# Summing quarters of softmax denominators on VectorE instead of TensorE, in a two-layer image kernel

## The chip, the cores and the metric

The kernel runs on one core of a Trainium2 chip, in float32. The metric is device time in microseconds (us), the median of several executions. TensorE (PE) multiplies matrices, VectorE (DVE) and GpSimd (POOL) do elementwise work, ScalarE (ACT) does activations and copies, SyncE (SP) issues the transfers. Each engine works through a queue of its own in a fixed order; a value that comes from another engine is waited for with a semaphore, and everything behind a waiting instruction in the same queue waits too.

## The reference

The input x has 4 images of 512 channels and 64x64 pixels (4096 pixels, called N). Layer 0 is self-attention with a residual, layer 1 an involution (a convolution whose weights differ from pixel to pixel) with a residual:

```
q = wq @ x + bq ; k = wk @ x + bk ; v = wv @ x + bv      # 128 channels each
attn = softmax(q^T k, axis=-1)                           # 4096 x 4096
x = wo @ (v @ attn^T) + bo + x                           # 512 channels
o = relu(W1 @ x * s1 + b1)                               # 128 channels
w = Ws @ relu(Wr @ o * sr + br) + bs                     # 8 groups x 49 taps
o = sum over 7x7 patch of w * patch(o)                   # per pixel and group of 16 channels
x = W3 @ o * s3 + b3 + x
```

## The kernel before

**Attention.** An image is worked in 8 blocks (c = 0 to 7) of 512 pixels as queries. A block has 32 steps, one for each 128 keys. In a step PE makes scores (`pss`) and ACT takes their exponentials straight from PSUM (`pt`, L797); two steps later PE multiplies the exponentials with the values into `po` (L820), and DVE adds them into a running sum `pacc` (L826 for the first, L828, and L831 for the last, whose result is `sums`). Nothing is divided until the block is over. After every step `chores` (L308) lets three generators go on by one step each: `finish_block` (what is left to do for the attention block before), `close_chunk` (the end of the involution for a block), and, paced by a planner's clock, `involution` (the taps). A bare `yield` in a generator is thus one step of the attention, a pause of n steps is n of them. The planner keeps a clock `pe` of the matmul work, and an estimate `free` of when DVE, POOL and the transfers will be done; `takes` (L211) books an instruction there. A tap is put into the program only where these estimates are not too far ahead of the clock.

**finish_block (L636 to 776).** `on` is the copy of `po` from PSUM. `sums` (128 partitions x 512 pixels) has to be summed over its partitions. DVE's `tensor_reduce` with a transpose (L654) gives `blocks`, 128 x 16: partition p = 32 i + a holds the part that quarter i of the partitions contributes to pixel a of each of the 16 groups of 32 pixels. The four quarters still have to be added. After a pause of 3 steps (L657) a matmul with `quads`, a matrix of repeated 32x32 identities, does this into a PSUM tile `pl` (L658 to 660), and every quarter receives the whole sum. DVE takes the reciprocal from PSUM into `rl` (L663), spreads it by a block transpose into a PSUM tile `spread` (L666), and multiplies `on` by it (L670). After another pause of 5 steps (L686) follow the four matmuls of the output projection `pwo` with their residual adds on DVE (L679), then the first 1x1 convolution of the involution (`p1`, ReLU to `o1`, L699), a transpose to pixel order (`o1t`, L732), its transfer to DRAM (`pix`), and the reduced weights (`pr`, `red`, L757). The last image (`late`) takes other waits, by the planner's clock, and computes the transposes on PE.

**Involution.** Sixteen units of 4 image rows for each image. A unit first makes its weights `pw` on PE. For each tap DVE multiplies a piece of the ring of image rows with the weights (`prod`, L427) and POOL adds the product into `acc` (L447); two folds on POOL end the unit (L462). `turn_unit` (L497) then transposes `acc` on DVE (`turned`, L508), writes it to DRAM (L517), and for every second unit reads it back as `accT`. `close_chunk` (L568) multiplies it by W3 in four matmuls `py` (L575), one every two steps; each is followed by the residual update of `x` on DVE (L577), and the transfer of the block to the output ends it (L586).

**PSUM.** The pool `ps` has two buffers for the tag "mm" (L127). All of `pl`, `spread`, `pwo`, `p1`, `pr`, `py` and the queries `pq` take turns in those two, in program order: a matmul into one of them waits until the reader of the tile two allocations earlier is done. The reader of `spread` is the product that makes `on` (L670); the reader of a `py` is the update of `x` (L577). Scores have two buffers of their own, `po`, `pacc` and `pw` one each. The tiles `pt` have five buffers, the products four.

The keys and values of an image (`keys_values`, L589) are made before its attention; while that happens the steps of the image before go on.

## Time and profile before

| what | value |
| --- | --- |
| times, three executions | 2587.20, 2587.73, 2589.54 us |
| median | 2587.73 us |
| profiled execution, its own time | 2587.14 us |
| its span | 2585.2 us |
| mean granted TensorE clock | 0.999 |
| PE busy | 2570.4 us |
| DVE busy | 1862.6 us |
| POOL busy | 1825.2 us |
| ACT busy | 838.2 us |
| `blocks` reduce (L654), one | 711 ns |
| reciprocal of 128x16 from PSUM (L663), one | 252 ns |
| spread (L666) and product (L670), one each | 716 and 674 ns |

An engine's busy time is what its instructions took; a share of the span near 100% means that the engine sets the time wherever it does not wait. Most of what happens here is cyclic: a step of the attention holds one score and one value product on PE, and the generators add their instructions between the steps. So one looks for the few places where PE waits, and for what DVE and POOL are doing just before them.

### The profile page before, as it was taken

What the parts mean: (1) busy time and instruction counts of PE and PEld (TensorE: products, weight loads), DVE (VectorE), ACT (ScalarE), POOL (GpSimd) and SP (SyncE); (2) the same over time, 40 slices, a digit from 0 to 9 for tenths busy, and PEclk for the clock granted to TensorE, in tenths of its full rate; (3) what the DMA queues carried; (4) which work ended last, traced back from release to release, by engine and by line L of the source; (5) the groups of instructions that cost most, each with busy time, mean ns of one, the idle gap of its engine ahead of it and who ended that gap; (6) DMA issues with size and microseconds to landing.
All of it is one profiled execution on the core that took longest, in us unless ns stands there. A gap on an engine that the chain in (4) does not pass through costs nothing.

```text
span 2585.2 us, 24342 instructions
## 1 busy us (share of the span) xinstructions
PE 2570.4 (99%) x7367; PEld 1229.3 (48%) x7367; DVE 1862.6 (72%) x2678; ACT 838.2 (32%) x1386; POOL 1825.2 (71%) x1207
## 2 busy tenths in 40 slices
PE   9999999999999999999999999999999999999998
PEld 7444444445544444444554444444465444444476
DVE  0347778887585777888667667878857678787888
ACT  1333333332233333333223333333322333333331
POOL 0006788877881778888786368888788567887887
PEclk9999999999999999999999999999999999999999
DMA  6033233445615343234661434433364431332343
GB/s 238 1 74 62 58 77 83 98 102 148 151 60 114 64 102 69 68 81 99 166 153 41 108 69 96 102 70 92 79 181 112 110 90 47 90 78 61 78 95 101
DMA packets 209049, 243.36 MB, mean 94 GB/s; under 512 B 109640, under 2 KB 129040, under 8 KB 208784
## 3 DMA queue, kind: packets, MB, share of 16 engines
q1 hardware_dynamic: 208480, 241.39, 38.9%
q8 instruction: 59, 0.97, 0.2%
q14 instruction: 78, 0.64, 0.1%
q10 hardware_dynamic: 432, 0.36, 0.1%
HBM read 192.65 MB, written 49.06 MB: 93 GB/s over the span
## 4 chain that ended last, share of the span: by engine, by line
PE 92%; POOL 4%; DVE 3%; issue 1%; ACT 0%; DVEq 0%; POOLq 0%
PE pss L255 32%; PE po L255 31%; PE pv L255 4%; PE pk L255 4%; PE pq L255 4%; PE p L255 4%; PE pwo L255 4%; PE py L255 4%; POOL acc L447 4%; PE pw L255 2%; DVE prod L427 1%; DVE pacc L828 1%; PE pr L255 1%; PE pa L259 1%; POOL acc L462 0%
## 5 line engine op out<-in xcount | busy, mean ns | idle before, releaser
L447 POOL TENSOR_TENSOR acc<-acc,prod 128x768 f32<-128x768 f32 (+3 forms) x1052 | 1682.8, 1617 | 737.9 <-DVE prod L427 694.6
L255 PE MATMUL pss<-q,k 128*128 128x512 f32 (+1 forms) x2112 | 1055.7, 584 | 0.0
L255 PE MATMUL po<-pt,v 128*128 128x512 f32 (+1 forms) x2112 | 1047.3, 580 | 0.0
L797 ACT ACTIVATE pt<-pss 128x512 f32<-128x512 f32 x1024 | 611.1, 597 | 1242.6 <-PE pss L255 1188.8
L427 DVE TENSOR_TENSOR prod<-ring,pw 128x768 f32<-128x768 f32 (+3 forms) x1086 | 874.7, 840 | 46.0 <-POOL acc L447 44.9
L828 DVE TENSOR_TENSOR pacc<-pacc,pt 128x512 f32<-128x512 f32 x958 | 664.8, 694 | 237.9 <-ACT pt L797 209.9
L255 PEld LDWEIGHTS po<-pt,v 128*128 128x128 f32 x2112 | 398.8, 190 | 480.9 <-issue 460.4
L255 PEld LDWEIGHTS pss<-q,k 128*128 128x128 f32 x2112 | 391.4, 190 | 466.8 <-issue 462.0
L508 DVE STREAM_TRANSPOSE turned<-acc 128x256 f32<-128x256 f32 x48 | 21.4, 445 | 217.9 <-POOL acc L462 217.9
L255 PE MATMUL py<-accT,wt 128*128 128x512 f32 (+1 forms) x256 | 130.1, 590 | 4.5 <-DVE x L577 4.5
L255 PE MATMUL pwo<-on,wt 128*128 128x512 f32 (+1 forms) x264 | 128.6, 580 | 0.1
L462 POOL TENSOR_TENSOR acc<-acc 128x512 f32<-128x512 f32 x122 | 121.4, 995 | 9.6
L255 PEld LDWEIGHTS pv<-wt,x 128*128 128x128 f32 x1024 | 119.6, 192 | 15.3 <-issue 15.1
L577 DVE SCALAR_TENSOR_TENSOR x<-py,vec,x 128x512 f32<-128x512 f32 (+2 forms) x136 | 96.4, 711 | 36.2 <-PE py L255 35.7
L255 PE MATMUL pv<-wt,x 128*128 128x128 f32 x1024 | 120.2, 275 | 0.0
L255 PE MATMUL p<-x,wt 128*128 128x512 f32 (+1 forms) x264 | 119.3, 580 | 0.0
L255 PE MATMUL pk<-x,wt 128*128 128x512 f32 x256 | 117.1, 596 | 0.0
L706 ACT ACTIVATE x<-x,vec 128x512 f32<-128x512 f32 (+1 forms) x132 | 92.9, 706 | 74.2 <-PE p L255 58.1
L255 PE MATMUL pq<-x,wt 128*128 128x512 f32 (+1 forms) x264 | 115.3, 579 | 0.0
L679 DVE SCALAR_TENSOR_TENSOR x<-pwo,bo,x 128x512 f32<-128x512 f32 (+1 forms) x132 | 95.1, 727 | 21.3 <-PE pwo L255 19.9
L427 DVE TENSOR_TENSOR acc<-ring,pw 128x1024 f32<-128x1024 f32 (+1 forms) x85 | 78.7, 945 | 15.6 <-PE pw L255 15.6
L255 PEld LDWEIGHTS pq<-x,wt 128*128 128x128 f32 x264 | 50.1, 190 | 59.7 <-issue 56.4
(74 smaller groups left out, 727.0 us busy)
## 6 DMA issues: line engine op xcount, KB each, us to landing
x<-x_dram SPq DMA_DIRECT2D x55, 1024.0 KB, 5.7
ring<-pix SPq DMA_DIRECT2D x74, 448.0 KB, 7.0
ring<-pix SPq DMA_DIRECT2D x24, 1344.0 KB, 9.7
out_dram<-x SPq DMA_DIRECT2D x31, 1024.0 KB, 4.5
ring<-pix SPq DMA_DIRECT2D x24, 896.0 KB, 10.5
ring<-pix SPq DMA_DIRECT2D x30, 672.0 KB, 10.9
ring<-pix SPq DMA_DIRECT2D x6, 2240.0 KB, 19.5
pix<-o1t SPq DMA_DIRECT2D x192, 32.0 KB, 1.7
```

The source lines that it names most:

```text
L255: return nc.tensor.matmul(o, lhsT=lhsT, rhs=rhs, start=start, stop=stop)
L259: nc.tensor.matmul(o, lhsT=lhsT, rhs=ident, start=start, stop=stop, is_transpose=True)
L427: product = (nc.gpsimd if maker == "pool" else nc.vector).tensor_tensor(made.rearrange("p t d (g c) -> p t d g c", g=G), image.rearrange(" ...
L447: nc.gpsimd.tensor_tensor(acc[:, these, d0 : d0 + n, :], acc[:, these, d0 : d0 + n, :], prod[:, :nt, :n, :], ALU.add,)
L462: nc.gpsimd.tensor_tensor(acc[:, :, :n, :], acc[:, :, :n, :], acc[:, :, n : 2 * n, :], ALU.add)
L508: nc.vector.transpose(blocks.rearrange("p (t k q) -> p t k q", t=NT, q=TB), acc[:, :, 0, :].rearrange("p t (k q) -> p t k q", q=TB),)
L577: nc.vector.scalar_tensor_tensor(xt[:, t, :], py, v1(V_S3 + t), xt[:, t, :], ALU.mult, ALU.add)
L679: nc.vector.scalar_tensor_tensor(xt[:, t, :], pw, bo[:, t : t + 1], xt[:, t, :], ALU.add, ALU.add)
L706: nc.scalar.activation(xt[:, t, :], xt[:, t, :], AF.Identity, bias=v1(V_B3 + t))
L797: nc.scalar.activation(pt, pss, AF.Exp)
L828: nc.vector.tensor_tensor(paccs[k], paccs[k], pt, ALU.add)
```

## The change

For the first three images the four quarters are added on DVE, and the matmul `pl` and the reciprocal from PSUM go. The first 16 columns of the `spread` tile in PSUM serve as scratch (`other`): `blocks` is copied there, then four additions of 32 partitions x 16 columns each make `pairs` (quarter i plus quarter i^1), `pairs` is copied to the scratch, two additions of 64 partitions x 16 columns make the full sum in `rl`, and the reciprocal is taken in place in SBUF. The spread over the scratch follows as before. The pause of 3 steps before this stays, the pause before the projection becomes 6 steps instead of 5. The planner is told of one more microsecond of DVE work. A new tile `blocks2` with two buffers holds the pairs. The last image is as before.

```
         blocks = work2.tile([P, CH // TB], F32, tag="blocks", name=f"blocks_{name}")
+        blocks2 = work2.tile([P, CH // TB], F32, tag="blocks2", name=f"pairs_{name}")
...
         yield from pause(free["dve"], 3)
-        pl = ps.tile([P, CH // TB], F32, tag="mm", name=f"pl_{name}")[:, : n // TB]
-        for i in range(CH // n):
-            mm(pl, quads, blocks[:, i * n // TB : (i + 1) * n // TB], i == 0, i == CH // n - 1)
         row = (b * N + c * CH + off) // TB
         rl = rls[:, row : row + n // TB]
-        nc.vector.reciprocal(rl, pl)
+        if late:
+            pl = ps.tile([P, CH // TB], F32, tag="mm", name=f"pl_{name}")[:, : n // TB]
+            for i in range(CH // n):
+                mm(pl, quads, blocks[:, i * n // TB : (i + 1) * n // TB], i == 0, i == CH // n - 1)
+            nc.vector.reciprocal(rl, pl)
 
         spread = ps.tile([P, CH], F32, tag="mm", name=f"spread_{name}")[:, :n]
+        if not late:
+            cols = n // TB
+            other, pairs = spread[:, :cols], blocks2[:, :cols]
+            nc.vector.tensor_copy(other, blocks)
+            for i in range(P // TB):
+                mine, next_ = (slice(j * TB, (j + 1) * TB) for j in (i, i ^ 1))
+                nc.vector.tensor_tensor(pairs[mine], blocks[mine], other[next_], ALU.add)
+            nc.vector.tensor_copy(other, pairs)
+            for i in range(2):
+                mine, next_ = (slice(j * 2 * TB, (j + 1) * 2 * TB) for j in (i, i ^ 1))
+                nc.vector.tensor_tensor(rl[mine], pairs[mine], other[next_], ALU.add)
+            nc.vector.reciprocal(rl, rl)
+            takes("dve", 1.0)
         nc.vector.transpose(
...
         if not direct:
-            yield from pause(spreads, 5)
+            yield from pause(spreads, 6)
             yield from residual()
```

## The prediction

> **What bounds the kernel now.** I read the page first (busy time, then the chain that ended last), then what PE waited for, then the timeline around the places that touch the change.

> ```profile
> PE 2570.4 (99%) x7367; PEld 1229.3 (48%) x7367; DVE 1862.6 (72%) x2678; ACT 838.2 (32%) x1386; POOL 1825.2 (71%) x1207
> ...
> PE 92%; POOL 4%; DVE 3%; issue 1%; ACT 0%; DVEq 0%; POOLq 0%
> ```

> PE sets the time: 99% busy. A microsecond of PE work taken away comes off the end, and work added to DVE is free as long as no PE instruction has to wait for it. How seldom it waits now, the waits by engine say:

> ```profile
> PE py L255 <- DVE x L577: 4.7, 5, 1.2
> PE pa L259 <- DVE prod L427: 1.6, 4, 0.7
> ```

> In total, number of times, longest. The first line is for the most part one place that comes back in three images (at 381, 1013 and 1645 us). The timeline at the first:

> ```profile
> 379.24 0.65 PE L255 MATMUL pr<-o,wt 128*64 128x256 f32 x4
> ...
> 380.22 0.74 DVE L577 SCALAR_TENSOR_TENSOR x<-py,vec,x 128x512 f32<-128x512 f32 x1
> ...
> 381.02 1.12 PE L255 MATMUL py<-accT,wt 128*128 128x512 f32 x2 [1.12 <-DVE x L577]
> ...
> 382.36 0.93 PE L255 MATMUL pw<-wt,red 33*128 33x392 f32 x4 [0.22 <-DVE prod L427]
> ```

> The second `py` of chunk 1 wants the buffer of its predecessor two allocations back, whose `x` DVE updates only at 380.22, and the `pw` behind it starts late as well. From the `pr` on, 1.12 us and about 0.5 us are lost: about 1.68 us here, 5.0 us over three images.

> Now what the change removes, in the PE timeline, and its DVE rows by form:

> ```profile
> 128.33 1.02 PE L255 MATMUL po<-pt,v 128*128 128x512 f32 x2
> 129.19 0.29 PE L255 MATMUL pl<-blocks,quads 128*128 128x16 f32 x2
> 129.33 1.10 PE L255 MATMUL pss<-q,k 128*128 128x512 f32 x2
> 130.27 1.02 PE L255 MATMUL po<-pt,v 128*128 128x512 f32 x2
> ```

> ```profile
> L508 DVE STREAM_TRANSPOSE turned<-acc 128x256 f32<-128x256 f32 x48 | 21.4, 445 | 217.9 <-POOL acc L462 217.9
> ...
> L663 DVE RECIPROCAL rls<-pl 128x16 f32<-128x16 f32 x31 | 7.8, 252 | 11.5 <-PE pl L255 11.4
> ...
> L848 DVE TENSOR_TENSOR bo<-pb,vec 128x4 f32<-128x4 f32 x1 | 0.2, 164 | 64.5 <-PE pb L255 64.5
> ```

> A score or value product holds PE for 0.86 us (128.33 to 129.19). From `pl` to the `po` behind the next score are 1.08 us instead of 0.86: `pl` costs 0.22 us, though it has only 16 columns. The first DVE row is the one to remember: all 48 `turned` transposes found POOL's folds not ready, 4.5 us each, with everything behind them in DVE's queue standing still.

> **The change part by part.** The sum is made against the profiled execution (2587.14 us: span 2585.2 and 1.94 around it), 0.6 us under the median.

> *Removed on PE:* 24 `pl` (3 images by 8 blocks) by 0.22 us = 5.4 us, with certainty nearly. The reciprocal is no longer waiting for it: of the 11.4 us of idle DVE time 24/31 go, 8.8 us, off PE's path.

> *Added on DVE:* per block two copies and six additions of 16 columns. The nearest row is the 128x4 addition from PSUM, 164 ns; the reciprocal of 128x16 takes 252. I take 0.175 us each, 8 x 0.175 = 1.4 us a block, 34 us over 24 blocks, with ends 0.15 (1.2 us) and 0.25 (2.0 us). DVE is idle for 720 us of the span, so none of it costs by itself; it counts only where DVE's end of a block decides a `mm` buffer.

> [...] In DVE's rows a successor starts 0.08 us before the end of the instruction ahead (740.91 + 0.45 against 741.28 below). [...]

> *Moved:* a block now allocates one `mm` buffer fewer and waits one step (1.72 us) longer before the projection, and the planner counts 1.0 us more of DVE. Following the issue order, POOL's order is unchanged, SP's transfers are the same in number (those of `pix`, `turned`, `accT` and the output move with their steps), but taps and units come later against the attention, and the `py` of chunks 3 and 6 come 6 to 7 steps later. Transfers: the x load issued at the image boundary keeps some 1 to 3 us before PE needs it, by 5.7 us from issue to landing; cost 0, upper end 3 x 3 us. In image 3 from its third block on, the order on every engine is that of before.

> *F, the wait of 5.0 us, goes.* In the new order seven rather than four us of other work stand between the two `py` of chunk 1 (6.86 against 3.95). The update of `x` needs about 4 us less than that. So -5.0; lower end 0 if DVE is 4 us later. What is late next are three new places.

> *G, chunk 6 at the border between images (twice: images 0 to 1, 1 to 2).* The `mm` order there is now py_6_0, py_6_1, spread, py_6_2, py_6_3. So py_6_2 waits for the `x` of py_6_1, and py_6_3, two steps behind, for the `on` of block 0. DVE's queue has ahead of that: the transpose of unit 14, last `pacc`, `sums`, reduce, `x` of py_6_0, `pacc` copy, `pacc`, copy and three additions, `x` of py_6_1; then the weight product of unit 15 and two taps (3 x 1.2 us), the addition, `x` of py_6_2, copy, sums, reciprocal, spread and product among three `pacc`. The timeline of before shows what unit 14 does to this queue:

> ```profile
> 733.14 1.50 DVE L828 TENSOR_TENSOR pacc<-pacc,pt 128x512 f32<-128x512 f32 x2
> 740.91 0.45 DVE L508 STREAM_TRANSPOSE turned<-acc 128x256 f32<-128x256 f32 x1 [6.27 <-POOL acc L462]
> 741.28 0.71 DVE L577 SCALAR_TENSOR_TENSOR x<-py,vec,x 128x512 f32<-128x512 f32 x1
> ```

> 6.27 us of standing still, without a loss on PE, as no buffer was wanted. Now unit 14 starts later by its taps, and POOL (about 30 us a unit) ends its folds later, just when the block ends. Worked back from the moment that py_6_2 wants to start, on a PE that runs undisturbed: unit 13's first addition can begin 65.2 us earlier, behind the moved update of a chunk 5 tile; the unit takes POOL 31.8 us, 3.9 us pass until the first product of unit 14 is there, which takes 30.2: 65.9. The folds end 0.7 us too late. Behind them stand 0.45 + 0.69 + 0.69 + 0.71 + 0.75 + 0.68 + 0.69 + 0.7 + 0.75 = 6.1 us: py_6_2 starts about 7.0 us late (6.8 and the hop between engines). From there py_6_3 has 4.3 us of PE work ahead of it, DVE 3.8 + 5.7 = 9.5 us: another 5.2. Late end: 12.2. If the folds are done in time, py_6_2 is on time (py_6_1 begins 4.3 us before it and its update is done 1.8 us later) and only py_6_3 waits: 9.5 us from there against 2.5 + 4.3, that is 2.7. I take 9.5 of 2.7 to 12.2, nearer the late end, since DVE arrived before the folds in 48 cases of 48. Twice: 19.0.

> *A, block 6 to 7 (three images).* The order is spread_6, py_3_0, py_3_1: py_3_1 waits for `on` of block 6. On time DVE has it 1.8 us before. Here unit 8's transpose stands ahead; at the same place before, DVE waited 5.5 us for it (521.4 to 526.9). Moved later by the shift of the taps, `on` comes 2.1 to 5.5 us late. Ends 0 and 5.5, I take 3.0, three times: 9.0.

> *I, start of image 3.* The `pl` of its first block is kept, and its buffer needs the `x` of py_6_0, behind the same unit 14. 0.3 if on time, 8.7 late (5.8 and two smaller waits behind); I take 5.0.

> Sum: -5.4 - 5.0 + 19.0 + 9.0 + 5.0 = +22.6, so 2587.14 + 22.6 = 2609.7 us, +0.9%.

> **The rivals.**

> *Folds in time (not slower).* Then G is 2 x 2.7, A 0, I 0.3: -10.4 + 5.7 = -4.7, 2582.4. It decides whether the `turned` of units 8 and 14 return before the block's reduce is due. For it: the planner places taps only as far as it believes POOL to be behind by some us, and delays taps further. Against: 217.9 us of DVE idle on 48 transposes.

> *All arrives.* Only the removed matmuls and F, no new wait: -10.4, 2576.7. G's `on` speaks against it: even on time it is 2.7 late, unless the two taps ahead are 2.4 us later.

> *Half of it.* A on time, G about 7 each, I 5: -10.4 + 14 + 5 = +8.6, 2595.7.

> [...]

> **How the numbers follow.** Forecast 0.50, half 0.16, folds in time 0.14, all arrives 0.10, beyond 2621 0.10. A measurement tells this kernel from no change at about 0.2%, 5.2 us: below 2582.5 is faster. Half of "folds in time" and all of "all arrives" lie there, as a part of F and G varies: 0.15. The other half and a part of "half": 0.15 within; slower 0.70. Range 2580 (into folds in time) to 2621. As both signs are in it: the forecast alone has 2600 to 2620.

> **What would show it.** The reciprocal from PSUM stays for the last image's blocks alone, 7 of 128x16; `pl` falls from 70 PE instructions to 22 (two each); 192 new small rows on DVE take 0.15 to 0.25 us. PE's waits: F's three gone; `py` waiting for DVE's `x` and for `on` at the two borders, near 755 and 1390 us, 5 to 12 us each; `py` waiting for `on` three times between blocks 6 and 7, 2 to 5 us. L508's idle still about 4 us each. It is wrong if PE's total of waits stays below 6 us, which would mean that the folds were in time, or if the removed matmuls were covered already (PE busy then falls by less than 5).

## The result, and the profile after

The changed kernel takes 2612.81 us (median of 6 runs, 2612.18 to 2613.84), the kernel before 2587.77 us. The ratio is 1.0096, with a 95% interval of 1.0083 to 1.0109: 25 us slower, where 2609.7 was forecast. The profiled execution has a span of 2612.0 us against 2585.2, 26.8 us more.

The busy times of the changed kernel, from the first part of its page:

```profile
PE 2576.8 (99%) x7319; PEld 1228.8 (47%) x7319; DVE 1895.7 (73%) x2870; ACT 838.8 (32%) x1386; POOL 1824.7 (70%) x1207
```

PE has 48 instructions fewer and is busy 6.4 us longer, so some of its passes must be slower. DVE has 192 instructions more and 33.1 us more work. What PE waited for (total, times, longest):

```profile
PE py L255 <- DVE x L577: 11.3, 4, 4.9
PE py L255 <- DVE on L685: 7.9, 3, 2.6
PE pl L255 <- DVE x L577: 4.0, 1, 4.0
PE pw L255 <- DVE prod L427: 2.7, 3, 0.9
```

The old wait at chunk 1 is gone, and new ones have come at the three places that the prediction names: the border between images (twice 4.9), between blocks 6 and 7 (three times 2.6), and the start of image 3 (4.0). Three of 0.9 us at `pw` were not foreseen. The border between images 0 and 1, in the timeline of DVE, GpSimd and PE:

```profile
755.74 2.07 POOL L462 TENSOR_TENSOR acc<-acc 128x512 f32<-128x512 f32 x2
...
757.84 0.45 DVE L508 STREAM_TRANSPOSE turned<-acc 128x256 f32<-128x256 f32 x1 [8.14 <-POOL acc L462]
758.21 0.67 DVE L843 TENSOR_TENSOR pacc<-pacc,pt 128x512 f32<-128x512 f32 x1
758.98 0.69 DVE L846 TENSOR_TENSOR sums<-pacc,pt 128x512 f32<-128x512 f32 x1
759.71 0.71 DVE L655 TRANSPOSE_TENSOR_REDUCE blocks<-sums 128x16 f32<-128x512 f32 x1
760.34 0.71 DVE L577 SCALAR_TENSOR_TENSOR x<-py,vec,x 128x512 f32<-128x512 f32 x1
...
762.57 0.53 DVE L674 TENSOR_TENSOR pairs<-blocks,spread 32x16 f32<-32x16 f32 x3
763.12 0.75 DVE L577 SCALAR_TENSOR_TENSOR x<-py,vec,x 128x512 f32<-128x512 f32 x1
...
763.93 2.08 PE L255 MATMUL py<-accT,wt 128*128 128x512 f32 x2 [4.94 <-DVE x L577]
765.79 1.91 PE L255 MATMUL pss<-q,k 128*128 128x512 f32 x2
767.50 1.64 PE L255 MATMUL po<-pt,v 128*128 128x512 f32 x2
```

Unit 14's transpose stops DVE for 8.14 us until GpSimd's folds are done, and everything for the end of the block and for `x` queues behind it. Over the whole kernel DVE stands before the 48 transposes for 200.6 us, less than the 217.9 us before the change: what costs here is the place of a wait, not the sum of the waits. PE's next projection needs a buffer that the `x` update at 763.12 frees. And a second thing follows: the `py`, the score and the value product behind the wait take 1.86, 1.71 and 1.48 us until the next one, instead of 0.86. PE runs at half its pace. The granted clock of the stretches around it says so too (columns: stretch and its length; busy time of PE, weight load, DVE, ACT and POOL with counts; granted clock; DMA share; GB/s):

```profile
715.00:758.00 43.00, 42.06 (x103) 18.11 (x102) 29.18 (x47) 13.22 (x22) 38.21 (x31) 1.00 0.08 20
758.00:770.00 12.00, 7.06 (x12) 2.88 (x11) 11.53 (x22) 1.19 (x2) 3.71 (x2) 0.72 0.08 12
770.00:800.00 30.00, 30.00 (x71) 13.26 (x71) 24.65 (x34) 9.81 (x16) 25.00 (x14) 1.00 0.20 71
```

The account of the 26.8 us, the new waits from the rows above and the rest from the intervals between successive PE passes, less what a pass takes undisturbed: the matmuls of the quarters -5.3, chunk 1's wait with its `pw` -4.6; new waits +24.5 (9.9 at the borders, 7.9 between blocks 6 and 7, 4.0 at image 3, 2.7 at `pw`; the other 1.4 of the first row lies in the tail, the end of the last image, as before); slow passes behind five of the six larger waits +11.5 (2.5, 3.0, 1.6, 1.7, 2.6). That makes 26.1; 0.7 is not assigned.

### The profile page after: what moved, and what is told of

Its sections match the earlier page's. It is cut to its first block, busy times and chain, and to the rows that moved or that the text cites. A ratio compares the mean times of both kernels' runs of the same rounds, so it can differ in the third digit from the quotient of the medians.

```text
span 2612.0 us, 24480 instructions
## 1 busy us (share of the span) xinstructions
PE 2576.8 (99%) x7319; PEld 1228.8 (47%) x7319; DVE 1895.7 (73%) x2870; ACT 838.8 (32%) x1386; POOL 1824.7 (70%) x1207
## 4 chain that ended last, share of the span: by engine, by line
PE 87%; POOL 6%; DVE 3%; issue 3%; DMA 0%; ACT 0%; SPq 0%; POOLq 0%; DVEq 0%
PE pss L255 30%; PE po L255 29%; POOL acc L447 5%; PE pv L255 4%; PE p L255 4%; PE pwo L255 4%; PE pk L255 4%; PE py L255 4%; PE pq L255 4%; PE pw L255 2%; DVE prod L427 1%; DVE pacc L843 1%; PE pr L255 1%; POOL acc L462 1%; PE pa L259 1%
## 5 line engine op out<-in xcount | busy, mean ns | idle before, releaser
L255 PE MATMUL pss<-q,k 128*128 128x512 f32 (+1 forms) x2112 | 1058.8, 586 | 0.0
L255 PE MATMUL po<-pt,v 128*128 128x512 f32 (+1 forms) x2112 | 1049.8, 581 | 0.0
L427 DVE TENSOR_TENSOR prod<-ring,pw 128x768 f32<-128x768 f32 (+3 forms) x1086 | 879.6, 841 | 68.4 <-POOL acc L447 66.0
L255 PEld LDWEIGHTS po<-pt,v 128*128 128x128 f32 x2112 | 400.3, 191 | 482.9 <-issue 465.0
L255 PEld LDWEIGHTS pss<-q,k 128*128 128x128 f32 x2112 | 395.5, 191 | 479.7 <-issue 473.4
L508 DVE STREAM_TRANSPOSE turned<-acc 128x256 f32<-128x256 f32 x48 | 21.4, 446 | 200.6 <-POOL acc L462 200.6
L255 PE MATMUL py<-accT,wt 128*128 128x512 f32 (+1 forms) x256 | 133.7, 605 | 18.9 <-DVE x L577 11.1
L255 PEld LDWEIGHTS pv<-wt,x 128*128 128x128 f32 x1024 | 121.0, 192 | 22.7 <-issue 22.4
L255 PE MATMUL pwo<-on,wt 128*128 128x512 f32 (+1 forms) x264 | 128.6, 580 | 0.1
L462 POOL TENSOR_TENSOR acc<-acc 128x512 f32<-128x512 f32 x122 | 121.6, 996 | 9.6
L577 DVE SCALAR_TENSOR_TENSOR x<-py,vec,x 128x512 f32<-128x512 f32 (+2 forms) x136 | 96.2, 710 | 43.4 <-PE py L255 42.5
L255 PE MATMUL pv<-wt,x 128*128 128x128 f32 x1024 | 122.8, 276 | 0.0
L255 PE MATMUL p<-x,wt 128*128 128x512 f32 (+1 forms) x264 | 119.3, 580 | 0.0
L255 PE MATMUL pk<-x,wt 128*128 128x512 f32 x256 | 117.1, 593 | 0.4 <-DMA x<-x_dram 0.3
L255 PE MATMUL pq<-x,wt 128*128 128x512 f32 (+1 forms) x264 | 115.9, 582 | 0.0
L427 DVE TENSOR_TENSOR acc<-ring,pw 128x1024 f32<-128x1024 f32 (+1 forms) x85 | 78.8, 946 | 15.9 <-PE pw L255 15.6
L255 PEld LDWEIGHTS py<-accT,wt 128*128 128x128 f32 x256 | 47.9, 194 | 74.0 <-issue 53.0
```

Of the source, the lines that this page charges most:

```text
L255: return nc.tensor.matmul(o, lhsT=lhsT, rhs=rhs, start=start, stop=stop)
L427: product = (nc.gpsimd if maker == "pool" else nc.vector).tensor_tensor(made.rearrange("p t d (g c) -> p t d g c", g=G), image.rearrange(" ...
L462: nc.gpsimd.tensor_tensor(acc[:, :, :n, :], acc[:, :, :n, :], acc[:, :, n : 2 * n, :], ALU.add)
L508: nc.vector.transpose(blocks.rearrange("p (t k q) -> p t k q", t=NT, q=TB), acc[:, :, 0, :].rearrange("p t (k q) -> p t k q", q=TB),)
L577: nc.vector.scalar_tensor_tensor(xt[:, t, :], py, v1(V_S3 + t), xt[:, t, :], ALU.mult, ALU.add)
```

## The experiments

### Which part moves the work: booking, pause, or the small instructions

The theory, called 'order' in what follows: the loss comes from where the taps and projections of the involution stand against the ends of the blocks. The rival: the small instructions make DVE late by their own time. Three kernels take the change apart, a fourth books half.

Without the planner's extra microsecond:

```
             nc.vector.reciprocal(rl, rl)
-            takes("dve", 1.0)
```

> All of the change but the planner's extra microsecond of VectorE. The order of taps and of the projections of the involution then stays that of the kernel before (chunk 6 of image 0 begins behind step 23 of the next block 0, not behind step 31). Theory 'order' (the loss comes from work that the booking moves onto the block border): the two new places, between blocks 6 and 7 and at the borders between images, do not wait; 2587.8 - 5.2 for the 24 matmuls, F's 4.6 stays or grows by a little as VectorE has 1.4 us more a block: 2582 to 2586. Rival 'small instructions' (the loss comes from the 34 us that they add on VectorE): as slow as the changed kernel, 2605 to 2613.

Measured: 2581.95 us (2581.57 to 2582.75), ratio to before 0.9977 (0.9967 to 0.9987). With all the small instructions and the longer pause in it, it is faster than the kernel before by 5.6 us. Its span is 2579.8; PE's busy time and its waits for `py`:

```profile
PE 2565.9 (99%) x7319; PEld 1224.0 (47%) x7319; DVE 1896.7 (74%) x2870; ACT 839.9 (33%) x1386; POOL 1824.6 (71%) x1207
```

```profile
PE py L255 <- DVE x L577: 4.7, 7, 1.2
```

DVE is as busy as in the changed kernel, and PE's waits are those of before in sum (4.7). What is left is the removed matmuls: 5.4 us of span.

The booking alone, in the kernel before:

```
         nc.vector.reciprocal(rl, pl)
+        if not late:
+            takes("dve", 1.0)
```

> The kernel before with nothing but one more microsecond booked for VectorE per block of the first three images: no instruction added or removed. Theory 'order': chunk 6 moves from step 23 to step 29 of the next image's first block, chunk 3 from step 30 to 26 of block 6; F goes (-4.6), the border waits come by: 2592 to 2610. Rival 'small instructions': as before, 2585 to 2590.

Measured: 2600.09 us, ratio 1.0047 (1.0030 to 1.0063), with not one instruction added. At the borders `py` now waits for the reciprocal of the quarters, again behind unit 14's transpose (what PE waited for, and DVE's and PE's rows of the timeline):

```profile
PE py L255 <- DVE rls L663: 10.2, 2, 5.1
```

```profile
752.84 0.45 DVE L508 STREAM_TRANSPOSE turned<-acc 128x256 f32<-128x256 f32 x1 [5.41 <-POOL acc L462]
...
762.40 0.25 DVE L663 RECIPROCAL rls<-pl 128x16 f32<-128x16 f32 x1
...
762.71 2.07 PE L255 MATMUL py<-accT,wt 128*128 128x512 f32 x2 [5.06 <-DVE rls L663]
```

The pause alone, in the kernel before:

```
-            yield from pause(spreads, 5)
+            yield from pause(spreads, 6)
```

> The kernel before with a pause of 6 instead of 5 steps ahead of the output projection, nothing else. Theory 'order through the booking': no place moves but the projections by one step: 2586 to 2590. Rival 'the pause' (one step more moves the whole involution behind the block border): 2600 to 2613.

Measured: 2587.31 us, ratio 0.9997 (0.9987 to 1.0007): nothing. So a number in the planner's books, which makes no engine work, costs 12.5 us alone, and taking it out of the changed kernel turns a loss of 25 us into a gain of 5.6. The prediction had named three sources of the shift (a buffer fewer, a step longer, the booking) without telling them apart; of these the booking is the one that moves the taps by itself. The order of PE's rows shows it for chunk 6: its first `py` comes behind step 23 of the next block 0 in the kernel before and in the runs without the booking, and behind step 29 with the booking alone. In the changed kernel it is step 31: the longer pause adds to the shift once the booking is there.

Half the booking:

```
-            takes("dve", 1.0)
+            takes("dve", 0.5)
```

> The changed kernel with 0.5 us booked instead of 1.0. Chunk 1 keeps the place that took F's wait away, chunk 6 begins behind step 25 of block 0 and is through before the border, chunk 3 behind step 25 of block 6. Theory 'order': both gains (-5.2 and -4.6) and no border wait: 2577 to 2582. Rival 'small instructions': 2603 or more.

Measured: 2590.95 us (2588.49 to 2592.5), ratio 1.0014 (1.0004 to 1.0024). That missed: neither 2577 to 2582 nor 2603. The waits of `py` at the borders and between blocks 6 and 7 are gone, and others have come:

```profile
PE pw L255 <- DVE prod L427: 5.8, 3, 1.9
PE pwo L255 <- DVE on L685: 2.5, 2, 1.4
```

Three times the weights of a unit wait for the last products of the unit before, since `pw` has a single buffer. The expectation had followed three known places only, and not what else a moved unit runs into.

### What DVE stands behind

> The changed kernel in which GpSimd leaves out the two folds that end each unit of the first three images (so the sum over the tap rows is incomplete there); every other instruction and the planner's booking stand where they stood. GpSimd's last work ahead of a unit's transpose gets 2.07 us shorter, and each unit can begin that much earlier. Theory 'VectorE stands behind the transpose that waits for the folds': at the border between images the wait of 4.9 us falls by at least 2.07, with the unit ahead also shorter by 4 to nothing; the wait between blocks 6 and 7 (2.6) falls below 0.6; with the slow passes behind them gone too: 2580 to 2597. Rival 'the projections stand too close to each other, whoever is ahead of them': the waits stay, 2608 to 2613.

```
+                if b == B - 1:
                   for n in (2, 1):
                     nc.gpsimd.tensor_tensor(
```

Measured: 2587.97 us, ratio to before 1.0000 (0.9990 to 1.0009), so 24.8 us of the loss are gone with 2.07 us a unit off GpSimd, within what was expected. PE's waits:

```profile
PE py L255 <- DVE on L686: 3.5, 3, 1.2
PE py L255 <- DVE x L578: 2.9, 4, 1.2
PE pw L255 <- DVE prod L427: 2.7, 3, 0.9
PE py L255 <- DVE rls L666: 1.4, 1, 1.4
```

The border's 4.9 fell to about 0.75 (2.9 less the 1.4 of the tail, halved) and the 2.6 between blocks 6 and 7 to 1.2 (below 0.6 was expected). With no wait left of 2 us or more (the longest is 1.4), no passes are slow either: the mean granted clock of the profiled execution is 1.000, against 0.994 in the changed kernel. DVE's standing behind GpSimd's last work for a unit is thus shown to carry the loss. Whether it is the 2.07 us just ahead of the transpose or the earlier start of every unit, this run does not tell; DVE still waits before all 48 transposes, for 124.9 us instead of 200.6. The `pw` waits stayed at 2.7.

### The price of the small instructions

Twice the additions, no booking:

```
-            for i in range(P // TB):
+            for i in [*range(P // TB)] * 2:
+                if i == 0:
+                    nc.vector.tensor_copy(other, blocks)
...
-            for i in range(2):
+            for i in [0, 1] * 2:
+                if i == 0:
+                    nc.vector.tensor_copy(other, pairs)
...
-            takes("dve", 1.0)
```

> The change without the booking, with the two copies and six additions done twice (the same values again): 192 more instructions on VectorE, by the rows of the changed kernel 0.167 to 0.172 us each, 33 us. The order of taps and projections is that of the run without the booking. Theory 'order': VectorE has the room, so no more than its waits at chunk 1 and a few small ones grow: 2582 to 2588. Rival 'small instructions': the doubled ones cost what the first ones would have, 2595 or more.

Measured: 2622.19 us, ratio 1.0133 (1.0116 to 1.0150): 40 us over the run without booking, more than the 33 us that the doubled instructions last. That misses the theory's 2582 to 2588 and lies in the rival's range, and the profile says how it comes. PE's waits, and DVE around block 3 of image 0:

```profile
PE pwo L255 <- DVE on L686: 25.0, 11, 6.1
```

```profile
347.09 0.25 DVE L681 RECIPROCAL rls<-rls 128x16 f32<-128x16 f32 x1
...
350.07 0.45 DVE L508 STREAM_TRANSPOSE turned<-acc 128x256 f32<-128x256 f32 x1 [2.73 <-POOL acc L462]
350.44 0.68 DVE L682 STREAM_TRANSPOSE spread<-rls 128x512 f32<-128x512 f32 x1
...
351.61 0.67 DVE L686 TENSOR_TENSOR on<-on,spread 128x512 f32<-128x512 f32 x1
...
352.33 2.07 PE L255 MATMUL pwo<-on,wt 128*128 128x512 f32 x2 [6.12 <-DVE on L686]
```

The same place without the doubling:

```profile
340.64 0.71 DVE L680 STREAM_TRANSPOSE spread<-rls 128x512 f32<-128x512 f32 x1
...
341.84 0.67 DVE L684 TENSOR_TENSOR on<-on,spread 128x512 f32<-128x512 f32 x1
342.43 0.70 DVE L842 TENSOR_TENSOR pacc<-pacc,pt 128x512 f32<-128x512 f32 x1
...
347.13 0.45 DVE L508 STREAM_TRANSPOSE turned<-acc 128x256 f32<-128x256 f32 x1 [4.00 <-POOL acc L462]
```

The small additions depend on each other, and the other work of DVE is queued in between, so twice the chain reaches from 338.06 to 347.34 us in the queue, 9.3 us for 2.8 us of copies and additions. So the spread falls behind unit 3's transpose, which the whole chain just preceded without the doubling. My expectation counted DVE's idle time as room; the room is only up to the next transpose. So the claim 'the small instructions are hidden' holds for the amount in the change and not for twice that amount.

### The pause, with the additions there

The change without booking and with the old pause:

```
-            takes("dve", 1.0)
...
-            yield from pause(spreads, 6)
+            yield from pause(spreads, 5)
```

> The quarters on VectorE alone: neither the booking nor the longer pause. Theory 'order': as the run without the booking, the projections one step earlier, and 'on' has 8 steps instead of 9 from the block's end: 2580 to 2586. Rival 'the sixth step is needed because VectorE's chain is longer now': pwo waits for 'on' by up to 1.7 us in many of the 24 blocks, 2590 to 2610.

Measured: 2592.64 us (2584.01 to 2594.01), ratio 1.0014 (1.0005 to 1.0024): 10.7 slower than with the pause of 6, above the expected 2580 to 2586, though no `pwo` waits for `on`, as the rival had it. It is chunk 1 again:

```profile
380.65 0.74 DVE L577 SCALAR_TENSOR_TENSOR x<-py,vec,x 128x512 f32<-128x512 f32 x1
...
381.45 1.12 PE L255 MATMUL py<-accT,wt 128*128 128x512 f32 x2 [2.08 <-DVE x L577]
```

The wait of 1.12 us of the kernel before has become 2.08, three times, and each is followed by slow passes (1.7, 3.3 and 3.3 us). Most of the loss is these passes: of the ten runs nine have a granted clock of 0.996 to 0.998 and take 2589.78 to 2594.01 us, and the tenth, with 0.999, takes 2584.01, inside the expected range. With the pause of 6, `pr` comes behind this `py` instead of ahead of it (at 382.18, the `py` at 378.08 without a wait); the next `py` waits 1.0. So the sixth step is worth nothing in the kernel before and about 10 us once the additions are on DVE without the booking.

The changed kernel, booking and all, with the old pause (same edit of the pause alone):

> The changed kernel with the old pause of 5 steps. Chunk 6 begins behind step 29 of the next block 0 instead of 31, chunk 3 behind step 26 of block 6 instead of 5 of block 7. Theory 'order': the wait between blocks 6 and 7 goes (3 x 2.8 and its slow passes, 11 in all), the one at the border stays in some form, 2593 to 2605. Rival 'small instructions': 2605 to 2613 whatever the pause.

Measured: 2592.06 us, ratio 1.0016 (1.0006 to 1.0026). The wait between blocks 6 and 7 is gone and the one at the border stays:

```profile
PE py L255 <- DVE x L577: 9.0, 4, 3.8
```

It is 1 us below the expected range; chunk 3 now begins behind step 26 of block 6, ahead of the block's end, and chunk 6 behind step 29, as with the booking alone. So with the booking the sixth step costs 20.8 us (2612.81 against 2592.06), and the loss of 25 us needs both: with the additions, the pause of 6 without the booking gives -5.6 us against the kernel before, and the booking with the pause of 5 gives +4.4.

### Whose buffer it is

The prediction had the last projection of the border wait for `on`, as `spread` holds the other buffer. The trace has no such wait: in the changed kernel that `py` starts at 770.70, `on` at 772.02. As `spread` keeps its buffer until `on` has read it, this `py` must have had the other one, that of the `py` just before it. So the two buffers do not always take turns in program order, as the description of the kernel and the prediction had it. Here the scratch gets a tile of its own:

```
         if late:
...
+        else:
+            pl = ps.tile([P, CH // TB], F32, tag="mm", name=f"pl_{name}")
         spread = ps.tile([P, CH], F32, tag="mm", name=f"spread_{name}")[:, :n]
...
-            other, pairs = spread[:, :cols], blocks2[:, :cols]
+            other, pairs = pl[:, :cols], blocks2[:, :cols]
```

> The changed kernel with the scratch in a PSUM tile of its own, allocated where the quarters' matmul had its tile; same instructions. At the border the buffers then go to py_6_0, py_6_1, scratch, spread, py_6_2, py_6_3 in turn, so that the third and fourth projection stand behind the chain of small additions and 'on' themselves. Theory 'a buffer's reader behind the transpose sets PE's waits': the border wait becomes longer than 4.9 (one py for the scratch's last addition, the next for 'on'), 2615 to 2630. Rival 'PSUM turns do not matter, VectorE is late as a whole': 2610 to 2615.

Measured: 2612.6 us, ratio 1.0097 (1.0082 to 1.0113), as the changed kernel. The wait at the border has another releaser:

```profile
PE py L255 <- DVE rls L680: 10.6, 2, 5.3
```

The third projection waits for the last small addition, 5.3 us instead of 4.9, and it stands three steps later in the program. The second wait that was expected, of the fourth projection for `on`, did not come: `on` is done at 772.11, and the projection begins at 772.36, directly behind the score ahead of it. The time missed the theory's 2615 to 2630 and lies in the rival's 2610 to 2615, while the releaser of the wait agrees with the theory. So this run does not decide between them; that every wait is a matter of PSUM's turns is not shown.

### A version that beats both

Booking for block 3 alone, which moves chunk 1 by one step and leaves the other places where they were:

```
-            takes("dve", 1.0)
+            if c == 3:
+                takes("dve", 1.0)
```

> The change with the microsecond booked for block 3 alone. Chunk 1 moves by one step (from step 21 to 22 of block 4), all later places stay as in the kernel before. Theory 'order': what is left of chunk 1's wait (1.2 and what its pw lost, three times) goes or shrinks, no border wait: 2578 to 2582. Rival 'any booking pushes the units behind a block border': 2588 or more.

Beside it, on the same chip, the run without booking again:

> The run without the booking again, beside the one with the booking for block 3: 2581 to 2583 by either theory.

Measured: 2578.68 us (2578.20 to 2579.52), ratio 0.9966 (0.9953 to 0.9978), and 2582.81 us, ratio 0.9980 (0.9971 to 0.9989). PE's waits with the booking for block 3:

```profile
PE py L255 <- DVE x L577: 2.2, 4, 1.2
```

Chunk 1's waits are gone; what is left is a wait of about 0.4 at each border and the 1.4 of the tail. So with another booking the additions come within 2 us of what the prediction's rival 'all arrives' gave (2576.7).

## Why the prediction was right, and where not

The time came within 3.1 us of the forecast, but the terms are not all as predicted.

- **The removed matmuls, -5.4:** 5.3 by the PE intervals, and 5.4 of span in the run without booking.
- **Chunk 1, -5.0:** -4.6. Right, by moving.
- **The borders, 9.5 each:** 7.4 and 8.0, made of other parts. The folds ended at 757.81 (755.74 + 2.07), 1.0 us before `py_6_2` was wanted (the `po` ahead begins at 757.97, and takes 0.86), not 0.7 after; the row of work behind them took 6.1 as counted (757.84 to 763.87 is 6.0), so `py_6_2` came 5.1 us late (4.9 of them idle by the profile) and not 7.0. The second wait, 5.2 for `on`, did not come: the step that failed is the one that took PSUM's two buffers as strictly alternating (`py_6_3` began at 770.70, and `on` only at 772.02). In its place stand 2.5 to 3.0 us of slow passes, which no term had.
- **Blocks 6 to 7, 3.0 each:** a wait of 2.6 for `on` against the 3.0 forecast, plus 1.6 and 1.7 us of slow passes in two of the three.
- **Image 3, 5.0:** 4.0 and 2.6 of slow passes.
- **Not foreseen:** `pw` waiting 0.9 us three times.
- **Small additions:** 0.175 us was taken; they took 0.167 (32 partitions), 0.170 (64), and the copies 0.167 and 0.172, 1.34 us a block. In the changed kernel they follow each other without the overlap of 0.08 us that larger ones show (from 762.57 on three, each beginning 0.17 to 0.18 us after the one ahead; the `x` update at 760.34 begins 0.08 us before the end of the reduce ahead of it, 759.71 + 0.71). The runs do not show why; by these rows it is worth 8 x 0.08 = 0.6 us a block at most.
- **The cause of the shift:** left among three; it is the booking, and the longer pause on top of it. That the folds stand ahead was the main argument, and taking them out shows it.

The likeliest case was thus right in mechanism (VectorE's queue behind the folds). That its sum came out so near is luck: 33.0 us of new waits were forecast at the three places and 21.8 came, and the 11.5 us of slow passes and 2.7 us at `pw`, which no term had, nearly make up for it.

## What to carry to other kernels

In a kernel whose bound engine is 99% busy, a change of place can cost more than a change of work (here 24.5 us of new waits against 5.3 us of matmuls removed): ask first which in-order queue has an instruction that always waits (here 48 transposes, 4.5 us each before the change), and whether the moved work lands behind it. A number in a planner's estimates is part of the program; try the change with the estimate left alone (here 2581.95 us against 2612.81). Idle time of a helper engine was no room for a dependent chain that did not end before that engine's next long wait (here 2.8 us of small instructions, spread over 9.3 us of the queue, and 40 us on the kernel).

## What was not expected of the hardware

Behind the longer waits PE's passes of 512 columns take 0.85 us instead of 0.43 for a while (in the changed kernel the two of the score at 765.79 take 1.71 us, the two at 768.98 take 0.86). Over the profiles of twelve kernels here, the tail left out, counting the interval by which PE was late and the extra time of the passes behind it: of 27 waits between 0.9 and 1.7 us none was followed by slow passes, of 15 between 1.9 and 2.8 us ten were, and of 13 from 3.9 to 6.3 us all. The extra time of the passes of 512 columns was 1.4 to 3.4 us. The same wait of 2.78 us at the same place of the three images brought 1.6, 0 and 1.7 us.

```profile
553.70:557.11 3.41, 1.06 (x3) 1.00 0.09 12
557.11:560.53 3.42, 3.14 (x4) 0.50 0.99 241
1195.40:1198.82 3.42, 1.50 (x4) 1.00 0.00 0
1198.82:1202.23 3.41, 2.72 (x7) 1.00 0.99 229
1837.12:1840.53 3.41, 0.91 (x3) 1.00 0.13 24
1840.53:1843.94 3.41, 3.29 (x4) 0.50 1.03 240
```

The wait at 1196 us falls across the end of a stretch, with 1.9 us of idle time in the first and 0.7 in the second, and nothing happens. In the other two places 2.35 and 2.5 us fall into one stretch, and the clock of the next is half. The other three falls came after 2.92, 3.41 and 2.68 us of idle time (the stretches from 758.50, 1400.21 and 2041.91 us on). In the twelve profiles, counting stretches at the full clock, it fell after all 20 with 2.09 us of idle time or more, after 3 of 9 with 1.44 to 1.93, and after none with less; what decides in between is not shown.

As a price: where a wait of about 2 us or more on PE brought slow passes here, they took 1.4 to 3.4 us on top; for the five such waits of the changed kernel that was 11.5 of its 26.8 us.
